# Setup of weight-derived constants moved from ahead of a branch into its arms

## The chip, the cores and the metric

The kernel runs on one core of one Trainium2 chip. The metric is the device time in microseconds of one execution. Three runs of the kernel before took 4162.62, 4162.65 and 4139.63 us (median 4162.62). The execution that the profile shows took 4152.3 us, and its span, from the first to the last instruction, is 4150.5 us. A core has five engines that are meant here by PE (TensorE, with PEld for its weight loads), DVE (VectorE), ACT (ScalarE), POOL (GpSimd) and SP (SyncE, which issues DMAs). ACT issues DMAs too, on a queue of its own.

## The reference

The input x is 32 sequences of 256 tokens with 256 features. The output is x + FFN(Cond(x, cond)).

Cond is a state-space block:

```python
xr, gate = split(x @ W_in.T)                 # 512 channels each
xc = silu(causal_conv4(xr + cond) + b_conv)
xn = layernorm(xc) * ln_g + ln_b
Bm, Cm, dt = split(xn @ W_xproj.T, 3)        # 16 states each
dt = tanh(dt @ W_dt.T + b_dt) * 0.01
Ad = 1 - dt * tanh(A_log)
Bd = Bm * min(norm(xn), 1)
h[t] = clip(h[t-1] * Ad[t] + Bd[t] * xn[t], -10, 10)
y[t] = Cm[t] . h[t] + D * xn[t]
out = (y * silu(gate)) @ W_out.T
```

FFN has two layers. Each is a local attention (8 heads of 64, a token shift, normalised and rotated q and k, window 128) and a gated feed-forward block with a layer norm, each with a residual.

## The kernel before, in words

The 32 sequences go in four groups of 8. For each group the state-space block is a scan over 256 steps in 8 chunks of 32. One step is one DVE instruction (`h`, line 576) on 128 rows (16 states by 8 sequences) and 512 channels. Its input `xrep` is a row of normalised x, spread over the 128 rows either by a DMA out of a DRAM scratch `xnd` (lines 465 and 550) or, in group 0 alone, by a small matmul (`bx`, line 558), and scaled on ACT by `beta` (line 569). After the scan of a group come two layers of attention and feed-forward. The scan of group g + 1 runs beside the layers of group g (`side_by_side`). Only group 0 has its scan to itself, at the start, and only the last group has its layers to itself, at the end.

The scan's work is written into an agenda: `at(s, what, ...)` puts a piece at step s, and the pieces are traced in the order of the steps, those of one step in the order in which they were added. Pieces of chunk c have steps around 32c, those that prepare it negative offsets. For chunk 0 the order is: load of x (`load_x`, step −43), input projection (`project`, −40 to −34, PE `ps_in`, line 333), convolution (`conv_in`, `conv_taps`, `conv_out`, −38 to −29; POOL does the first tap `acc`, line 369, DVE the others), the projections of the raw convolution output on the states (`raw_sums`, −26, PE `ps_raw` from `wx_sb`), the norm (`norm_turn` to `norm_out`, −24 to −12; statistics on DVE, the power of −0.5 on POOL at line 444, `xn` on ACT, gain and bias on POOL at lines 460 and 461, then the write to `xnd` and the square on ACT), `figures` and `figures_in` (−9 and −7, these read `wsum` and `wbias`), `decays` (−5, reads `a_sb`), then the steps from 0 on. `skip` multiplies with `dskip_sb` (line 618), `project_y` uses `w_out_sb`, and the gate's pieces use the second half of the input projection.

The written order is not the issue order. A planner orders each engine's instructions from dependencies, from the priority that the written order gives, and from its own estimate of when operands are there; an instruction that needs nothing can be issued well ahead of its place. `tc.keep_in_program_order` ties an instruction behind the one written before it on its engine in the same block. Buffers come from pools; tiles with one tag share that tag's buffers. `ap_` has the tags `rot` (4 buffers) and `swp` (3 buffers) of 128x512. In the scan of group 0 `rot` holds the tiles `xq`; both tags serve attention later. `ps_w` has 8 banks of PSUM.

Two versions of the program exist in one kernel, behind a test at run time. `bounded` is 1 when the scales of q and k are small enough to do without the maximum in the softmax; every engine reads it and takes one arm of `tc.If`. Nothing in an arm is issued ahead of that. Ahead of the test lies the setup. It loads the weights and constants, mostly on ACT's queue (`loaded`, lines 110 to 120), and computes from them:

- masks, selectors and identity matrices, from nothing (POOL and DVE);
- `a_sb` = −0.01 tanh(A_log) (lines 168 and 169), `w_out_sb` halved (line 172), `head_rows` (line 197);
- rotation tables `rc_sb` and `rs_sb` times the scales (lines 219 to 233, DVE, line 229);
- `bounded` (lines 235 to 244, DVE);
- `wx_sb`, which is W_xproj with W_dt folded into its last third and the norm's gain folded in: four times a transpose (line 258), a copy, a product with W_dt (line 262) and a copy (lines 256 to 265);
- `wsum` and `wbias`, the sums that let the norm be applied after the projection: six times a copy that repeats 16 columns 8 times (`wide`, 128x512, DVE, line 269), four matmuls with 2 columns (`tw`, line 272, two records each in the profile) and a copy (lines 267 to 280).

Of the kernel before, what the change touches and what calls it, by code (L numbers as in the profile page):

```python
# [10 lines left out]
FP = mybir.dt.float32  # L11
BF = mybir.dt.bfloat16
I32 = mybir.dt.int32
AF = mybir.ActivationFunctionType
ALU = mybir.AluOpType
AX = mybir.AxisListType
PSUM = bass.MemoryType.PSUM
DRAM = bass.MemoryType.DRAM

P = 128  # L20
S = 256
DM = 256
KM = DM // P
DI = 512
NC_ = DI // P
NS = 16
GB = 8
# [9 lines left out]
HEADS = 8  # L37
DH = 64
W = 128
NW = S // W  # L40
HID = 682
MCH = [(o, min(P, HID - o)) for o in range(0, HID, P)]
MREM = MCH[-1][1]
# [6 lines left out]
SCALES2 = 25.0  # L50


def bc(ap, axis, n):

    ap = ap.unsqueeze(axis)
    shape = list(ap.shape)
    shape[axis] = n
    return ap.broadcast_to(shape)
# [15 lines left out]
def kernel(  # L74
# [29 lines left out]
    nc = tc.nc  # L104
    B = xT.shape[2]
    L = wqkv.shape[1]
    NG = B // GB

    const = ctx.enter_context(tc.tile_pool(name="const", bufs=1))
    def loaded(src, shape, name, q=None):  # L110
        t = const.tile(shape, FP, tag=name, name=name)
        (q or nc.scalar).dma_start(out=t, in_=src)
        return t

    def per_state(src, name):
# [3 lines left out]
        nc.scalar.dma_start(out=t, in_=src)  # L119
        return t  # L120

    w_in_sb = loaded(w_inT, [P, KM, 2 * DI], "w_in_sb", nc.sync)
    cond_sb = loaded(condT, [P, NC_, B], "cond_sb")
    wc_sb = loaded(w_conv, [P, NC_, TAPS], "wc_sb")
    bconv_sb = loaded(b_conv, [P, NC_], "bconv_sb")
    lng_sb = loaded(s_ln_g.partition_broadcast(P), [P, DI], "lng_sb")
    lnb_sb = loaded(s_ln_b.partition_broadcast(P), [P, DI], "lnb_sb")
    dskip_sb = loaded(d_skip.partition_broadcast(P), [P, DI], "dskip_sb")
    w_out_sb = loaded(w_outT, [P, NC_, DM], "w_out_sb")
    flg_sb = loaded(f_ln_g, [P, L, KM], "flg_sb")  # L130
    flb_sb = loaded(f_ln_b, [P, L, KM], "flb_sb")
    b1_sb = loaded(b1, [P, L, 2, len(MCH)], "b1_sb")
    b2_sb = loaded(b2, [P, L, KM], "b2_sb")
    bdt_sb = per_state(b_dt, "bdt_sb")
    a_sb = per_state(a_log, "a_sb")

    ident = const.tile([P, P], FP, tag="ident", name="ident")
# [17 lines left out]
    for j in range(NJ):  # L155
# [9 lines left out]
    nc.gpsimd.memset(half, 0.5)  # L165


    nc.scalar.activation(a_sb, a_sb, AF.Tanh)
    nc.vector.tensor_scalar(a_sb, a_sb, -1.0, 0.01, ALU.mult, ALU.mult)


    nc.vector.tensor_scalar(w_out_sb, w_out_sb, 0.5, None, ALU.mult)

    mask_t = const.tile([P, 2 * W], BF, tag="mask_t", name="mask_t")
    ident_b = const.tile([P, P], BF, tag="ident_b", name="ident_b")
# [3 lines left out]
        out=mask_t[:, 0:W], in_=mask_t[:, 0:W], compare_op=ALU.is_ge, fill=MASKED_LOW,  # L181
# [3 lines left out]
        out=mask_t[:, W : 2 * W], in_=mask_t[:, W : 2 * W], compare_op=ALU.is_ge,  # L185
# [6 lines left out]
    head_rows = const.tile([P, HEADS, DH], FP, tag="head_rows", name="head_rows")  # L192
    for r in range(2):
        nc.gpsimd.memset(head_cols[:, r, r * 16 : (r + 1) * 16], 1.0)
    for h in range(HEADS):
        row = 32 * (h // 2) + 16 * (h % 2)
        nc.vector.tensor_copy(
            head_rows[:, h, :], ident[:, row : row + 1].broadcast_to([P, DH])
        )

    b1g_sb = const.tile([P, L], FP, tag="b1g_sb", name="b1g_sb")
    nc.scalar.dma_start(
        out=b1g_sb[DH : DH + MREM], in_=b1[0:MREM, :, 1, len(MCH) - 1]
    )

    bounded = const.tile([1, 1], I32, tag="bounded", name="bounded")

    rc_sb = const.tile([P, L, NW, 2, DH], FP, tag="rc_sb", name="rc_sb")
    rs_sb = const.tile([P, L, NW, 2, DH], FP, tag="rs_sb", name="rs_sb")


    wx_sb = const.tile([P, NC_, 4 * NS], FP, tag="wx_sb", name="wx_sb")

    wsum = const.tile([P, 3], FP, tag="wsum", name="wsum")
    wbias = const.tile([P, 3], FP, tag="wbias", name="wbias")
    with tc.tile_pool(name="setup", bufs=2) as setup, tc.tile_pool(
        name="setup_ps", bufs=2, space=PSUM
    ) as sps:

        for src, pos, dst in ((qk_scale, rot_c, rc_sb), (qk_scale_sw, rot_s, rs_sb)):  # L220
            tab = setup.tile([P, NW, 2, DH], FP, tag="tab", name="tab")
            nc.scalar.dma_start(out=tab, in_=pos)
            for l in range(L):
                sc = setup.tile([P, 2 * DH], FP, tag="qk_sc", name="qk_sc")
                nc.scalar.dma_start(
                    out=sc, in_=src[l].rearrange("a d -> (a d)").partition_broadcast(P)
                )
                for w in range(NW):
                    nc.vector.tensor_mul(
                        dst[:, l, w].rearrange("p a d -> p (a d)"),  # L230
                        tab[:, w].rearrange("p a d -> p (a d)"),
                        sc,
                    )

        sq = setup.tile([1, L, 2, DH], FP, tag="sq", name="sq")
        nc.scalar.dma_start(out=sq, in_=qk_scale.unsqueeze(0))
        nc.vector.tensor_mul(sq, sq, sq)
        big = setup.tile([1, L, 2], FP, tag="big", name="big")
        nc.vector.tensor_reduce(big, sq, AX.X, ALU.max)
        nc.vector.tensor_mul(big[:, :, 0], big[:, :, 0], big[:, :, 1])  # L240
        nc.vector.tensor_scalar(big[:, :, 1], big[:, :, 0], SCALES2, None, ALU.is_le)
        allb = setup.tile([1, 1], FP, tag="allb", name="allb")
        nc.vector.tensor_reduce(allb, big[:, :, 1], AX.X, ALU.min)
        nc.vector.tensor_copy(bounded, allb)

        wx0 = setup.tile([P, NC_, 3 * NS], FP, tag="wx0", name="wx0")
        nc.scalar.dma_start(out=wx0, in_=w_xT)
        wdt_sb = setup.tile([NS, NS], FP, tag="wdt", name="wdt_sb")
        nc.scalar.dma_start(out=wdt_sb, in_=w_dtT)
        gcol = setup.tile([P, NC_], FP, tag="gcol", name="gcol")  # L250
        nc.scalar.dma_start(out=gcol, in_=s_ln_g.rearrange("(c p) -> p c", p=P))

        cols = setup.tile([P, NC_, 2], FP, tag="cols", name="cols")
        nc.gpsimd.memset(cols[:, :, 0:1], 1.0)
        nc.scalar.dma_start(out=cols[:, :, 1], in_=s_ln_b.rearrange("(c p) -> p c", p=P))
        for c in range(NC_):
            td = sps.tile([P, P], FP, tag="td", name="td")
            nc.tensor.transpose(td[0:NS, :], wx0[:, c, 2 * NS : 3 * NS], ident)
            wdT = setup.tile([NS, P], FP, tag="wdT", name="wdT")
            nc.vector.tensor_copy(wdT, td[0:NS, :])  # L260
            td2 = sps.tile([P, P], FP, tag="td", name="td2")
            nc.tensor.matmul(td2[:, 0:NS], wdT, wdt_sb, start=True, stop=True)
            nc.vector.tensor_copy(wx0[:, c, 2 * NS : 3 * NS], td2[:, 0:NS])
        nc.gpsimd.memset(wx_sb, 0.0)
        nc.vector.tensor_mul(wx_sb[:, :, 0 : 3 * NS], wx0, bc(gcol, 2, 3 * NS))
        for i in range(3):
            for src, k, dst in ((wx_sb, 0, wsum), (wx0, 1, wbias)):
                wide = setup.tile([P, NC_, NS, GB], FP, tag="wide", name="wide")
                nc.vector.tensor_copy(wide, bc(src[:, :, i * NS : (i + 1) * NS], 3, GB))
                tw = sps.tile([P, 2], FP, tag="tw", name="tw")  # L270
                for c in range(NC_):
                    nc.tensor.matmul(
                        tw,
                        wide[:, c].rearrange("p n b -> p (n b)"),
                        cols[:, c, :],
                        start=(c == 0),
                        stop=(c == NC_ - 1),
                    )
                nc.vector.tensor_copy(dst[:, i : i + 1], tw[:, k : k + 1])
        nc.vector.tensor_add(wbias[:, 2:3], wbias[:, 2:3], bdt_sb)  # L280

# [1 line left out]
    for i in range(2):  # L285
        t = const.tile([P, NI * (P + GB)], FP, tag=f"ly{i}", name=f"ly{i}")
# [3 lines left out]
    def program(ctx, exact):  # L290
# [7 lines left out]
        ap_ = ctx.enter_context(tc.tile_pool(name="at", bufs=2, reuse_waits="tile"))  # L298
        aw = ctx.enter_context(tc.tile_pool(name="aw", bufs=3, reuse_waits="tile"))
        ps_w = ctx.enter_context(tc.tile_pool(name="psw", bufs=8, space=PSUM, reuse_waits="tile"))  # L300

        def bank(pool, tag, name):
            return pool.tile([P, DI], FP, tag=tag, name=name)

        def reorder(out, ps):

# [5 lines left out]
        def group_scan(g, ys):  # L312
# [13 lines left out]
            def at(s, what, *args):  # L326
                agenda.setdefault(s, []).append(partial(what, *args))
# [376 lines left out]
            at(-1, start)  # L704
            if alone:
                at(-30, spread_weights)
            for c in range(NCH):
                for t in range(CH):
                    at(c * CH + t, step, c, t)
# [136 lines left out]
        if exact:  # L846
# [4 lines left out]
                out=mask[:, 0:W], in_=mask[:, 0:W], compare_op=ALU.is_ge, fill=MASKED,  # L851
# [449 lines left out]
        for _ in group_scan(0, ys):  # L1301
            pass
# [5 lines left out]
        for g in range(NG):  # L1308
# [12 lines left out]
            at = state_at[0]  # L1321
# [119 lines left out]
```

## Time and profile before

| | |
|---|---|
| median of 3 runs | 4162.62 us (4139.63 to 4162.65) |
| profiled execution | 4152.3 us |
| its span | 4150.5 us, 51929 instructions |
| mean granted TensorE clock | 0.959 |
| PE / DVE / ACT / POOL busy | 91% / 63% / 44% / 41% |
| `bounded` written, arm's first instruction (SP) | 22.3 us, 22.9 us |
| first `ps_in` on PE | 37.3 us |
| first and last scan step of group 0 begin | 69.6 us, 464.1 us |

Busy shares are means over the whole span. In the scan of group 0 alone, POOL is busy for about 19 of 47 us per chunk and DVE for about 40. Every row of a timeline gives the start, the duration, the engine, the line, the operation with its result and its operands, the shapes, the number of instructions merged into the row, and in brackets the idle time of the engine before it and what ended it. A name with a q after the engine (ACTq, SPq) is the engine's sequencer, which issues DMAs. Windows give busy times of each engine in a stretch, then the granted clock, the share of the DMA engines and GB/s.

### The profile page before, as it was taken

The numbers are of one execution on the slowest core, as the hardware profiler recorded it, in microseconds if no ns is written. First come the engines' busy times: TensorE is split into PE (matmuls) and PEld (weight loads), VectorE is DVE, ScalarE is ACT, GpSimd is POOL, SyncE is SP. The second block draws the span as 40 slices with busy tenths as digits, with TensorE's granted clock in tenths as the row PEclk, the third lists the DMA queues.
The fourth block names the chain that finished last, engine by engine and source line by source line (L and its number), as shares of the span: only waits on it lengthen the run. The fifth ranks groups of instructions, "written<-read, shape, count | busy, mean of one in ns | idle before, by whom it ended". The sixth has DMA issues, their size and how long they took to land. (4 is left out here: it accounts for less than half of the span.)

```text
span 4150.5 us, 51929 instructions
## 1 busy us (share of the span) xinstructions
PE 3797.3 (91%) x18236; PEld 2008.9 (48%) x18236; DVE 2627.6 (63%) x4986; ACT 1810.9 (44%) x3345; POOL 1699.9 (41%) x1749
## 2 busy tenths in 40 slices
PE   5898898899989999899898999889998899999999
PEld 3333355544555455444455445554455545654653
DVE  5888567777766456767767636777776744434433
ACT  2655344545445334444544424454544533323331
POOL 3333265325543166423654136532554316513531
PEclk8988899999999999999999999999999999999999
DMA  4444312444335312444433421244433421000000
GB/s 118 123 113 113 80 44 72 128 120 119 92 84 146 81 44 76 114 111 120 106 88 113 124 65 44 75 127 119 119 90 91 139 77 37 8 14 22 1 11 32
DMA packets 257346, 353.10 MB, mean 85 GB/s; under 512 B 160867, under 2 KB 170420, under 8 KB 254900
## 3 DMA queue, kind: packets, MB, share of 16 engines
q1 hardware_dynamic: 172624, 337.67, 29.8%
q10 hardware_dynamic: 84452, 12.01, 1.9%
q8 instruction: 147, 2.41, 0.3%
q14 instruction: 123, 1.01, 0.1%
HBM read 314.49 MB, written 33.55 MB: 84 GB/s over the span
## 5 line engine op out<-in xcount | busy, mean ns | idle before, releaser
L576 DVE CUSTOM_DVE_ANT_0 h<-h,xrep,lim 128x512 f32<-128x512 f32 x1024 | 894.7, 874 | 82.5 <-PE y L588 23.3
L569 ACT ACTIVATE xrep<-xrep,beta 128x512 f32<-128x512 f32 x896 | 609.4, 716 | 771.2 <-DMA xrep<-xnd 702.6
L786 PE MATMUL ps_qkv<-wqkv_sb,res 128*128 128x512 f32 x1536 | 750.2, 628 | 32.5 <-ACT oT L1036 8.2
L810 POOL TENSOR_TENSOR rot<-rot,swp 128x512 f32<-128x512 f32 x256 | 327.4, 1279 | 655.1 <-DVE swp L807 597.8
L786 PEld LDWEIGHTS ps_qkv<-wqkv_sb,res 128*128 128x128 f32 x1536 | 290.5, 199 | 386.9 <-issue 304.9
L818 POOL TENSOR_TENSOR rn<-ss,neg_half 128x8 f32<-128x8 f32 x256 | 436.7, 1706 | 23.3 <-DVE ss L816 11.7
L802 DVE TENSOR_TENSOR rot<-ps_qkv,rc_sb 128x512 f32<-128x512 f32 x256 | 175.7, 686 | 393.3 <-ACT sq L799 392.9
L1145 PE MATMUL po_f<-ag,w_sb 128*128 128x512 f32 (+1 forms) x768 | 358.9, 618 | 21.6 <-DVE ag L1126 21.5
L588 PE MATMUL y<-h,ly 128*32 128x512 f32 x2048 | 362.0, 631 | 14.3 <-DVE h L576 13.1
L1116 PE MATMUL pa<-hT,w_sb 128*128 128x512 f32 (+1 forms) x896 | 364.0, 597 | 0.0
L1126 DVE SCALAR_TENSOR_TENSOR ag<-pa,b_sb,gl 128x512 f32<-128x512 f32 x192 | 143.5, 748 | 320.3 <-PE pa L1116 147.5
L1116 PE MATMUL pg<-hT,w_sb 128*128 128x512 f32 x640 | 309.8, 607 | 0.3 <-ACT gl L1124 0.3
L333 PE MATMUL ps_in<-xg,w_in_sb 128*128 128x256 f32 x1024 | 291.1, 414 | 12.8 <-issue 4.5
L819 POOL TENSOR_TENSOR rot<-rot,rn 128x512 f32<-128x512 f32 x256 | 280.1, 1094 | 19.0
L380 DVE SCALAR_TENSOR_TENSOR acc<-xr,wc_sb,acc 128x256 f32<-128x256 f32 x384 | 199.4, 523 | 111.1 <-POOL acc L369 108.5
L1079 POOL TENSOR_TENSOR rstd<-ve,neg_half 128x1 f32<-128x1 f32 x128 | 77.9, 609 | 467.3 <-DVE ve L1077 461.6
L333 PEld LDWEIGHTS ps_in<-xg,w_in_sb 128*128 128x128 f32 x1024 | 191.0, 201 | 156.0 <-issue 71.9
L1000 ACT ACTIVATE pT<-sc 128x512 f32<-128x512 f32 x384 | 206.1, 592 | 127.4 <-PE sc L991 114.0
L836 PE MATMUL ps_wo<-oT,wo_sb 128*128 128x256 f32 x1024 | 237.3, 385 | 0.0
L1145 PEld LDWEIGHTS po_f<-ag,w_sb 128*128 128x128 f32 (+1 forms) x768 | 135.4, 191 | 203.1 <-issue 133.5
L799 ACT ACTIVATE sq<-ps_qkv 128x512 f32<-128x512 f32 x256 | 148.1, 592 | 187.0 <-PE ps_qkv L786 141.5
L991 PE MATMUL sc<-qT,kT 64*128 64x128 f32 (+1 forms) x2048 | 227.1, 352 | 1.9 <-ACT kT L830 1.8
(152 smaller groups left out, 5615.2 us busy)
## 6 DMA issues: line engine op xcount, KB each, us to landing
xrep<-xnd SPq DMA_DIRECT2D x448, 512.0 KB
xnd<-xn SPq DMA_DIRECT2D x64, 256.0 KB
wqkv_sb<-in_wqkv_dram SPq DMA_DIRECT2D x8, 1536.0 KB
xd<-xnd SPq DMA_DIRECT2D x192, 64.0 KB
w_sb<-in_w_dram SPq DMA_DIRECT2D x8, 1364.0 KB
xg<-in_xT_dram SPq DMA_DIRECT2D x64, 128.0 KB
ys<-yo ACTq DMA_DIRECT2D x64, 128.0 KB
res<-ys SPq DMA_DIRECT2D x32, 256.0 KB
```

Of the source, the lines that this page charges most:

```text
L333: nc.tensor.matmul(ps, w_in_sb[:, k, ch * P : (ch + 1) * P], ck[c]["xg"][:, k], start=(k == 0), stop=(k == KM - 1),)
L569: nc.scalar.activation(bx, ck[c].pop(("bx", t), bx), AF.Copy, scale=ck[c]["beta"][:, t : t + 1])
L576: nc.vector._custom_dve(TENSOR_ADD_SAT, out=h_new, in0=state["h"], in1=bx, s0=ck[c]["lim"][:, 0, t : t + 1], s1=ck[c]["lim"][:, 1, t : t + 1],
L588: nc.tensor.matmul(ck[c]["y", hb][32 * q : 32 * q + 32, :], ly[hb % 2][:, 32 * t : 32 * t + 32], ck[c].pop(("h", hb * TB + t)), start=(i = ...
L786: nc.tensor.matmul(ps, res[b // 2][:, k, b % 2, t0 : t0 + W], wqkv_sb[:, k, a * DI : (a + 1) * DI], start=(k == 0), stop=(k == KM - 1),)
L810: nc.gpsimd.tensor_add(rot, rot, swp)
L818: nc.gpsimd.tensor_tensor(rn, ss, neg_half, ALU.pow)
L819: nc.gpsimd.tensor_mul(rot, rot, bc(rn, 2, DH))
L836: nc.tensor.matmul(po[:, d], wo_sb[:, c, d * P : (d + 1) * P], oT[:, c, :], start=(c == 0), stop=(c == NC_ - 1),)
L991: nc.tensor.matmul(banks[r][:, i, :], kT[rows, i0 + i, kw * W : (kw + 1) * W], qT[rows, i0 + i, kw * W :], start=False, stop=(i == n - 1),)
L1116: nc.tensor.matmul(ps[0:n, :], self.w1[:, k, half_ * HID + o : half_ * HID + o + n], self.h[j][:, k].rearrange("p b t -> p (b t)"), start= ...
L1145: nc.tensor.matmul(self.po[d], self.w2[r0 : r0 + n, m, d * P : (d + 1) * P], self.ag[m][r0 : r0 + n, :], start=(m == 0), stop=(m == len(MC ...
```

## The change

The test moves forward: the load of the scales and the chain that computes `bounded` come first, ahead of all other loads, with the load on SP's queue. Seven loads (`dskip_sb`, `w_out_sb`, the norms' and the feed-forward's constants) and all that the setup computes from weights, except `bounded`, move into the arms as pieces of the agenda of group 0. They get work tiles of `rot` and `swp` in place of the setup's own pool and PSUM banks of `ps_w`, whose pool of the setup goes.

| step | piece | engine |
|---|---|---|
| −43 | `load_w`: four loads, two fills | ACT queue, POOL |
| −34, −32 | `fold_1`, `fold_2`: the four transposes into one bank and one copy, four products and one copy, then `wx_sb` | PE, DVE |
| −28 to −18 | `widen_w`, six, 128x512 | POOL, in written order (before: DVE) |
| −27 to −17 | `sum_w`, six, four matmuls each, into one bank | PE |
| −19 | `decay_rate` | ACT, DVE |
| −16 | `load_later`: the seven loads | ACT queue |
| −14 | `sums_w`: two copies and an addition | DVE |
| 14 | `halve`, 128x1024 | POOL, in written order (before: DVE) |
| 30 | `load_tables`: six loads | ACT queue |
| 50 to 68 | `tables`, four, 128x256 each | POOL, in written order (before: eight on DVE) |
| 100 to 114 | `head_table`, eight, 128x64 | POOL, in written order (before: DVE) |

The removed parts of the setup are those that the list of the previous section names; the core of what is added:

```diff
+    bounded = const.tile([1, 1], I32, tag="bounded", name="bounded")
+    with tc.tile_pool(name="setup", bufs=1) as setup:
+        sq = setup.tile([1, L, 2, DH], FP, tag="sq", name="sq")
+        nc.sync.dma_start(out=sq, in_=qk_scale.unsqueeze(0))
...
+        nc.vector.tensor_copy(bounded, allb)
+
     w_in_sb = loaded(w_inT, [P, KM, 2 * DI], "w_in_sb", nc.sync)
...
-    dskip_sb = loaded(d_skip.partition_broadcast(P), [P, DI], "dskip_sb")
-    w_out_sb = loaded(w_outT, [P, NC_, DM], "w_out_sb")
-    flg_sb = loaded(f_ln_g, [P, L, KM], "flg_sb")
-    flb_sb = loaded(f_ln_b, [P, L, KM], "flb_sb")
-    b1_sb = loaded(b1, [P, L, 2, len(MCH)], "b1_sb")
-    b2_sb = loaded(b2, [P, L, KM], "b2_sb")
...
+        def constants(at):
+            tmp = {}
+            def work(tag, name, bufs):
+                return ap_.tile([P, HEADS, DH], FP, tag=tag, name=name, bufs=bufs).rearrange(
+                    "p h d -> p (h d)"
+                )
+            def load_w():
+                w = work("rot", "wx", 4)
...
+                nc.scalar.dma_start(out=tmp["wx"], in_=w_xT)
+                nc.scalar.dma_start(out=tmp["dt"], in_=w_dtT)
+                nc.scalar.dma_start(out=tmp["g"], in_=s_ln_g.rearrange("(c p) -> p c", p=P))
+                nc.scalar.dma_start(
+                    out=tmp["cols"][:, :, 1], in_=s_ln_b.rearrange("(c p) -> p c", p=P)
+                )
+                nc.gpsimd.memset(tmp["cols"][:, :, 0], 1.0)
+                nc.gpsimd.memset(wx_sb, 0.0)
+            def fold_1():
+                td = bank(ps_w, "w", "td")
+                for c in range(NC_):
+                    nc.tensor.transpose(
+                        td[0:NS, c * P : (c + 1) * P], tmp["wx"][:, c, 2 * NS :], ident
+                    )
+                wdT = work("swp", "wdT", 3)
+                nc.vector.tensor_copy(wdT[0:NS], td[0:NS])
...
+            def widen_w(i, k):
+                t = ap_.tile([P, NC_, NS, GB], FP, tag="swp", name="wide", bufs=3)
+                src = (wx_sb, tmp["wx"])[k]
+                tc.keep_in_program_order(
+                    nc.gpsimd.tensor_copy(t, bc(src[:, :, i * NS : (i + 1) * NS], 3, GB))
+                )
+                tmp["wide"] = t
...
+            def halve():
+                tc.keep_in_program_order(
+                    nc.gpsimd.tensor_scalar_mul(w_out_sb, w_out_sb, 0.5)
+                )
+            def load_tables():
+                tab, sc = work("swp", "tab", 3), work("swp", "qk_sc", 3)
...
+            def tables(i, l):
+                dst = (rc_sb, rs_sb)[i][:, l].rearrange("p w a d -> p w (a d)")
+                tc.keep_in_program_order(
+                    nc.gpsimd.tensor_mul(dst, tmp["tab"][:, i], bc(tmp["sc"][:, i, l], 1, NW))
+                )
...
+            at(-43, load_w)
+            at(-34, fold_1)
+            at(-32, fold_2)
+            for n in range(6):
+                at(-28 + 2 * n, widen_w, n // 2, n % 2)
+                at(-27 + 2 * n, sum_w, n // 2, n % 2)
+            at(-14, sums_w)
+            at(-19, decay_rate)
+            at(-16, load_later)
+            at(14, halve)
+            at(30, load_tables)
+            for n in range(2 * L):
+                at(50 + 6 * n, tables, n // L, n % L)
+            for h in range(HEADS):
+                at(100 + 2 * h, head_table, h)
...
             if alone:
                 at(-30, spread_weights)
+                constants(at)
```

## The prediction

> **What bounds the kernel now.** First the page, for the whole span:
>
> ```profile
> span 4150.5 us, 51929 instructions
> ...
> PE 3797.3 (91%) x18236; PEld 2008.9 (48%) x18236; DVE 2627.6 (63%) x4986; ACT 1810.9 (44%) x3345; POOL 1699.9 (41%) x1749
> ```
>
> TensorE is busy for 91% of the span, so work taken from VectorE or GpSimd in the middle of the program is worth nothing there. But the change rewrites the first microseconds, so the view that decides is the timeline from 0 to 130 us (start, duration, engine, line, operation):
>
> ```profile
> 17.14 0.32 ACTq L236 DMA_DIRECT2D sq<-in_qk_scale_dram  x1
> ...
> 20.11 0.41 DVE L237 TENSOR_TENSOR sq<-sq 1x256 f32<-1x256 f32 x1
> ...
> 22.13 0.13 DVE L244 CAST bounded<-allb 1x1 int32<-1x1 f32 x1
> ...
> 22.93 2.61 SPq L346 DMA_DIRECT2D xg<-in_xT_dram  x4
> ...
> 25.59 0.95 SPq L1195 DMA_DIRECT2D wqkv_sb<-in_wqkv_dram  x1
> ...
> 27.09 10.37 PE L272 MATMUL tw<-cols,wide 128*128 128x2 f32 x48 [1.23 <-issue]
> ...
> 37.32 6.03 PE L333 MATMUL ps_in<-xg,w_in_sb 128*128 128x256 f32 x16
> ...
> 45.85 1.33 POOL L369 TENSOR_SCALAR acc<-xr,wc_sb,bconv_sb 128x256 f32<-128x256 f32 x2
> ...
> 49.02 0.60 POOL L362 COPY xr<-carry 128x24 f32<-128x24 f32 x2 [1.84 <-DVE acc L380]
> ...
> 53.09 1.08 POOL L444 TENSOR_TENSOR stat<-ve,neg_half 128x1 f32<-128x1 f32 x2 [3.47 <-DVE ve L443]
> ```
>
> Two gates stand in a row. The arms open when `bounded` is written (22.26); its input was asked for only at 17.14, behind some twenty other loads on ACT's queue, and the arm's first instruction follows at 22.93. Then the first projection `ps_in` waits again, not for data: TensorE has 48 `tw` matmuls of the setup ahead of it. The DMA view of 24 to 26 us shows that its input was there by then, since the 2048 short packets of the first chunk's two `xg` loads are all in this stretch (counts are packets, MB, share):
>
> ```profile
> q1 hardware_dynamic: 2051, 0.26, 82.4%
> ```
>
> So `ps_in` could have begun near 26 and began at 37.3. From there to the first scan step is a chain of latencies (convolution, transpose, statistics, affine, write and re-read of `xnd`), as VectorE's timeline from 60 us and the busy times by window show (PE, PEld, DVE, ACT, POOL, clock, DMA share, GB/s):
>
> ```profile
> 69.62 0.81 DVE L576 CUSTOM_DVE_ANT_0 h<-h,xrep,lim 128x512 f32<-128x512 f32 x1
> ```
>
> ```profile
> 50.00:60.00 10.00, 1.62 (x8) 0.83 (x8) 2.27 (x9) 2.55 (x6) 6.08 (x6) 0.78 0.11 32
> 60.00:70.00 10.00, 7.95 (x28) 5.58 (x30) 5.91 (x21) 2.71 (x6) 4.43 (x11) 0.70 0.51 144
> ```
>
> TensorE is idle for 8.4 of the 10 us after 50: whatever shortens the way to 69.62 shortens the program.
>
> **The change, step by step**, against the profiled execution (4152.3 us, 1.8 around its span).
>
> 1. *The gate.* The load of `sq` takes the first place on SP, where `w_in` is issued now (0.74 us). Issue to use of `sq` was 20.11 − 17.14 = 3.0 us, an upper bound, VectorE having been busy until 20.1. That gives 3.7. The chain to `bounded` took 2.15 with other work between (1.4 by its rows alone), the arm 0.67 more: the arm opens near 6.2 to 6.6. The other engines are there: GpSimd's fills end at 3.9, less the two that move; ACT keeps 7 of its loads, whose issues end near 4.6 (the pause of 2.15 us that I see came behind the eighth); VectorE's remaining sums and copies, 1.9 us, fit while `sq` travels. Gain 22.9 − 6.4 = **16.5 us**.
> 2. *TensorE's queue.* `ps_in` waits for `xg`, 3.1 us after the arm's start by the row above. At 6.4 the last of `w_in`, `lng` and `lnb` and the moved `wx`, `g`, `cols` travel too, so I add 0.5: `ps_in` at 10.0, not 37.3. Steps 1 and 2 are **−27.3** in all. The bounds are −28.5 (nothing collides) and −22 (the fold's transposes are put ahead of `ps_in` and wait for `wx` among the weights' 4.2 MB).
> 3. *The fold on TensorE and VectorE.* 8 records of transposes (0.38) and 8 of products (0.38) cost at most 6 us if each stands alone, but now go in two batches with one round trip each, inside the lead-in, where TensorE is idle after `ps_in`. VectorE adds 0.28–0.45 + 0.2 + 0.36, about 1 us, between convolution taps that are the path. The 48 `tw` records (0.216 us apart) lie in TensorE's idle time; if they had no cover they would cost 10.4. Cost **+1**, ends 0 and +4.
> 4. *Six widening copies on GpSimd.* No row shows a GpSimd copy of 128x512. Below stands the fill of 128x544 (0.55), above the two-input 128x512 of L460 (1.26). Twice the one-input 128x256 of L369 (0.64) is 1.27; I take 1.1, nearest to the one-input row. They total 6.6, ends 3.3 and 7.6. By the order that the pins write, four stand behind the last `acc` and ahead of the first power, where GpSimd is idle from 47.2 to 53.1 but for 0.6: covered. The other two stand between the first power and the second half's affine, where GpSimd works back to back from 54.8 to 60: 2.2, less 0.6 of idle. Cost **+1.6**, ends 0 and +7.6 (no cover).
> 5. *ACT's loads.* The seven deferred loads took about 5 us to issue (0.45, 0.45, 0.34, 1.35, 0.93 for two, 1.43). They depend on nothing, and row L1195 shows that such loads go out as soon as the arm opens, whatever their place in the program. ACT idles until its first `th`, some 7 us behind `ps_in`; the four `wx` loads and these fill 6.7 of its 10. Cost **+0.5**, ends 0 and +5 (issued between `xn` and its square, on the path).
> 6. *In the scan that runs alone.* Halving 128x1024 (some 2.2 by the rows of 4), four 128x256 products (0.65) and eight head copies (0.2 each by L362) are 6.4 us on GpSimd, which is busy 19 of 47 us per chunk there and mostly waits for VectorE. Six table loads take ACT 2.5 us. Cost **+1**, ends 0 and +7. VectorE loses 3.7 us of setup rows that were ahead of both gates and are already counted.
>
> Sum: −27.3 + 1 + 1.6 + 0.5 + 1 = **−23 us**, ends −28.5 and about −10. From the profiled execution that is 4129; from the median of the runs (4162.62) 4140, from their lowest (4139.63) 4117. I say **4133**, between the first two.
>
> [...] The six copies: DVE does one in 0.42 us by its row L269, GpSimd's one-input row is 0.64 for half the size. [...] The clock: the 16 `ps_in` behind `tw` average 558 ns where the run's shortest is 379, so they were already slow. [...]
>
> **Rivals.**
>
> *The constants become the chain* (0.15). `wide`, `wdT` and the tables share the three `swp` buffers. If the tables' loads, which need nothing, take two of them at the arm's start and keep them, the copies run singly: 6 × (1.1 + 1.73 of `tw` + 0.3) = 19 us from the last `acc`, 10 behind `ps_in`, to 29, while `figures_in` needs the sums at 26 (63.5 − 37.3). With ACT's issues on the path too that is some 8 to 10 us lost: −13, 4139 by the profiled execution. For it: loads do float (L1195). Against: TensorE is free meanwhile.
>
> *The arms don't open early* (0.05): an engine reaches the branch late, as ACT did with its queue full, or one of its loads is held. At 12 us instead of 6.4, the gain is 17: 4135.
>
> *More than 1% faster* (0.13). The direct gain ends at 28.5 us, 0.7%. It needs runs like the lowest before: 4139.6 − 23 = 4117, or a start-up that is warm as well (from 80 to 90 us the clock is 0.68 and TensorE full: 3 us).
>
> *Slower* (0.06). One mechanism: no pin holds TensorE, ACT or VectorE, and the order of the later instructions is planned from the new start; if that order feeds the scan later, each step pays. The page has 82.5 us of idle time before the 1024 `h` steps, 0.08 us each. At 0.022 us more for each the 23 us are gone, at 0.063 the program is 1% slower: 4152 − 23 + 64 = 4193. For it: `h` waits 9.0 us for ACT's `xrep` in the first 600 us already. Against: the moved work is done before step 116 of the first 256, and the other three groups have the same instructions as before.
>
> The forecast itself has the rest, 0.61. The range reaches from the lowest base with most of the gain (4139.6 − 28.5 = 4111, and a little for the faster case) to the median with nothing gained: **4105 to 4163**. 1% of 4162.62 is 41.6 us, about what a measurement of this kernel can tell from no change; by the cases: faster 0.13, within 1% 0.81, slower 0.06.
>
> **What the profile afterwards would show.** Right: `bounded` near 6 us, the first `ps_in` near 10 with no `tw` ahead of it, the first `h` step near 45.4 (69.6 − 27.3 + 3.1, step 6 coming later), and the same distance from there to the end. Step 4 is right if GpSimd's copies are about 1.1 us and the first power follows the last `acc` by some 6 us. Step 5 is wrong if ACT's queue shows loads between `xn` and `sq_x`; the first rival is right if each `wide` waits for the `tw` before it. The slower case would show as more idle time before L576. I am wrong in sign if the distance from the first `h` step to the end grows by more than 23 us.

## The result, and the profile after

| | before | after |
|---|---|---|
| median of 12 runs each | 4159.07 us (4139.63 to 4167.02) | 4142.44 us (4132.39 to 4154.91) |
| ratio | | 0.9971, 95% interval 0.9953 to 0.9989 |
| profiled execution, its span | 4152.3 us, 4150.5 us | 4133.24 us, 4131.4 us |
| first `ps_in` | 37.32 us | 10.43 us |
| last `xc` ends | 50.25 us | 26.23 us |
| last `tp_x` ends | 51.62 us | 35.80 us |
| first scan step | 69.62 us | 54.51 us |

The change makes the kernel faster by 0.29%, some 12 us by the ratio and 16.6 by the medians. In a later comparison on one chip, with five runs of it, the ratio was 0.9965 (0.9952 to 0.9979), 15.6 us by the medians. The forecast was 23 us, a ratio of 0.9945: the direction held, and the size is beyond the interval. That the time itself, 4133, met the profiled execution (4133.24) is luck: this was the second fastest of the 12.

The page of the changed kernel, its first line and the busy times of the whole span, says nothing of this:

```profile
span 4131.4 us, 51897 instructions
...
PE 3798.7 (92%) x18236; PEld 2010.1 (49%) x18236; DVE 2621.9 (63%) x4953; ACT 1812.4 (44%) x3345; POOL 1716.0 (42%) x1768
```

TensorE is as busy as before (3797.3 us there); the 19 us are idle time that is gone. The timeline of the changed kernel from 3 to 56 us shows where it went and where some came back (start, duration, engine, line, operation; in brackets the idle time before it and what ended it):

```profile
3.83 0.14 DVE L134 CAST bounded<-allb 1x1 int32<-1x1 f32 x1
...
6.31 1.01 SPq L419 DMA_DIRECT2D xg<-in_xT_dram  x2
...
10.43 5.80 PE L406 MATMUL ps_in<-xg,w_in_sb 128*128 128x256 f32 x12 [10.43 <-DMA xg<-in_xT_dram]
...
20.37 0.35 DVE L283 TENSOR_TENSOR wx_sb<-wx 128x192 f32<-128x192 f32 x1
...
23.03 1.86 PE L300 MATMUL tw<-wx,wide 128*128 128x2 f32 x8 [3.42 <-POOL wide L289]
24.83 2.82 PE L472 MATMUL ps_raw<-xc,wx_sb 128*64 128x256 f32 x6
...
25.81 0.42 DVE L463 SCALAR_TENSOR_TENSOR xc<-th,acc 128x256 f32<-128x256 f32 x1 [0.55 <-ACT th L458]
...
27.57 1.87 PE L300 MATMUL tw<-wx,wide 128*128 128x2 f32 x8
29.30 0.88 PE L502 MATMUL tp_x<-ident,xc 128*128 128x128 f32 x3
29.98 3.41 PE L300 MATMUL tw<-wx,wide 128*128 128x2 f32 x16
33.25 0.88 PE L502 MATMUL tp_x<-ident,xc 128*128 128x128 f32 x3
34.06 1.12 PE L472 MATMUL ps_raw<-xc,wx_sb 128*64 128x256 f32 x2
35.11 0.69 PE L502 MATMUL tp_x<-ident,xc 128*128 128x128 f32 x2
...
35.62 1.30 DVE L512 BATCH_NORM_STATS2 st<-tp_x 128x6 f32<-128x512 f32 x2 [9.39 <-PE tp_x L502]
...
54.51 0.89 DVE L649 CUSTOM_DVE_ANT_0 h<-h,xrep,lim 128x512 f32<-128x512 f32 x1
```

Both gates are open: `bounded` is written at 3.97, the load of x leaves at 6.31, and `ps_in` begins at 10.43 with no `tw` ahead of it. But 32 of the 48 `tw` records now stand between the projection and the last transpose `tp_x`, and the first of them keeps TensorE waiting for a copy on GpSimd. TensorE kept to that order: `ps_raw`, which stands next, had its first `xc` at 18.83 and its `wx_sb` at 20.72 and begins at 24.83, behind the first eight, though TensorE idled for 3.42 us ahead of these. VectorE's statistics, which are the path, wait 9.39 us for the transposes. In the timeline of the kernel before, the same wait was 1.19:

```profile
49.43 0.82 DVE L390 SCALAR_TENSOR_TENSOR xc<-th,acc 128x256 f32<-128x256 f32 x2
...
50.96 0.66 PE L429 MATMUL tp_x<-ident,xc 128*128 128x128 f32 x4
...
51.44 1.29 DVE L439 BATCH_NORM_STATS2 st<-tp_x 128x6 f32<-128x512 f32 x2 [1.19 <-PE tp_x L429]
```

In numbers, from the first `ps_in` to the first scan step: 32.3 us before, 44.1 after. Of the 11.8 more, 2.9 lie ahead of the last `xc` (15.8 against 12.9), 8.2 between it and the last `tp_x` (9.6 against 1.4), and 0.7 behind that (18.7 against 18.0). So of the 26.9 us that the gates give, 15.1 are left at the first scan step.

### The profile page after: what moved, and what is told of

Read it like the earlier page. It is cut to its first block, busy times and chain, and to the rows that moved or that the text cites. A ratio compares the mean times of both kernels' runs of the same rounds, so it can differ in the third digit from the quotient of the medians.

```text
span 4131.4 us, 51897 instructions
## 1 busy us (share of the span) xinstructions
PE 3798.7 (92%) x18236; PEld 2010.1 (49%) x18236; DVE 2621.9 (63%) x4953; ACT 1812.4 (44%) x3345; POOL 1716.0 (42%) x1768
## 5 line engine op out<-in xcount | busy, mean ns | idle before, releaser
L892 POOL TENSOR_TENSOR rn<-ss,neg_half 128x8 f32<-128x8 f32 x256 | 437.2, 1708 | 23.2 <-DVE ss L890 11.8
L406 PE MATMUL ps_in<-xg,w_in_sb 128*128 128x256 f32 x1024 | 289.2, 411 | 21.6 <-DMA xg<-in_xT_dram 10.4
```

Of the source, the lines that this page charges most:

```text
L406: nc.tensor.matmul(ps, w_in_sb[:, k, ch * P : (ch + 1) * P], ck[c]["xg"][:, k], start=(k == 0), stop=(k == KM - 1),)
L892: nc.gpsimd.tensor_tensor(rn, ss, neg_half, ALU.pow)
```

## The experiments

The theory after the result, called O in what follows, was the order: the planner put the sums' matmuls ahead of the transposes in TensorE's queue, and the transposes wait behind them as `ps_raw` does (ready at 20.72, begun at 24.83). Its rival C was the clock: in the window from 20 to 40 us of the changed kernel the granted clock is 0.50, so that TensorE might have been late whatever the order.

**The gate alone.** The chain of `bounded` moves to the front of the kernel before; all else stays.

```diff
+    bounded = const.tile([1, 1], I32, tag="bounded", name="bounded")
+    with tc.tile_pool(name="gate", bufs=1) as setup:
+        sq = setup.tile([1, L, 2, DH], FP, tag="sq", name="sq")
+        nc.sync.dma_start(out=sq, in_=qk_scale.unsqueeze(0))
...
-        sq = setup.tile([1, L, 2, DH], FP, tag="sq", name="sq")
-        nc.scalar.dma_start(out=sq, in_=qk_scale.unsqueeze(0))
```

> The kernel before with one edit: the load and the chain of `bounded` stand first; all other setup stays ahead of the arms, on the engines where it was. My account (two gates in a row, steps 1 and 2 of the prediction): the arm's first instruction on SP comes near 6 us instead of 22.9, but TensorE still has the fold and the 48 `tw` records ahead of `ps_in`, so `ps_in` begins between 33 and 38 us and the first `h` step between 65 and 70; the time does not change by more than the runs scatter. Rival (the branch alone was the gate): `ps_in` begins near 21 us and the first `h` near 54, as in the changed kernel.

Measured: 4158.38 us in one run, beside 4155.85 of the kernel before. Its timeline:

```profile
3.47 0.14 DVE L133 CAST bounded<-allb 1x1 int32<-1x1 f32 x1
...
15.89 5.10 SPq L347 DMA_DIRECT2D xg<-in_xT_dram  x4
...
28.05 10.37 PE L273 MATMUL tw<-cols,wide 128*128 128x2 f32 x48 [1.23 <-issue]
38.29 5.22 PE L334 MATMUL ps_in<-xg,w_in_sb 128*128 128x256 f32 x16
...
70.61 0.81 DVE L577 CUSTOM_DVE_ANT_0 h<-h,xrep,lim 128x512 f32<-128x512 f32 x1
```

`bounded` is there at 3.6. SP asks for x only at 15.89, not near 6 as expected; why stays open. It makes no difference, since `ps_in` waits for the setup's matmuls as before. It begins at 38.29 and the first scan step at 70.61, both just above the ranges expected. The prediction's two gates stand in a row, and the first is worth nothing by itself. (The second alone was not run.)

**The sums behind the transposes.** On the changed kernel, the six `sum_w` are tied behind what is written before them on TensorE, none earlier than step −19, the second half of the norm. For that, three of the `wide` tiles go to the tag `rot`.

```diff
-                    nc.tensor.matmul(
+                    tc.keep_in_program_order(nc.tensor.matmul(
...
-                at(-27 + 2 * n, sum_w, n // 2, n % 2)
+                at(max(-19, -27 + 2 * n), sum_w, n // 2, n % 2)
```

> The changed kernel with the `sum_w` matmuls written at steps -19 and -17, behind the second `norm_turn`, and tied there in written order; three of the six `wide` tiles take `rot` buffers so that no copy waits for a sum. Theory O (order): the `tw` records stand ahead of the transposes `tp_x` in TensorE's queue and hold the norm back; here the last transpose ends 1 to 3 us behind the last `xc` instead of 9.6, and the first `h` step comes at 46 to 48 us instead of 54.5; the time falls by 7 to 8 us against the changed kernel, ratio to the kernel before near 0.995. Theory C (clock): the stage is long because TensorE runs at half clock from 20 to 50 us; then the transposes stay slow and the first `h` stays within 2.5 us of 54.5.

Measured: 4134.37 us, ratio 0.9943 (0.9929 to 0.9956). By the ratio that is 24 us below the kernel before, by the medians 21.5; the forecast had 23. Its timeline:

```profile
22.44 1.12 PE L508 MATMUL tp_x<-ident,xc 128*128 128x128 f32 x4
...
27.00 0.44 PE L508 MATMUL tp_x<-ident,xc 128*128 128x128 f32 x2
27.27 9.73 PE L305 MATMUL tw<-wx,wide 128*128 128x2 f32 x48
...
47.67 0.89 DVE L655 CUSTOM_DVE_ANT_0 h<-h,xrep,lim 128x512 f32<-128x512 f32 x1
```

All 48 records follow the last transpose, which ends at 27.4, 1.1 us behind the last `xc`. The first scan step is at 47.67, 6.8 us earlier than with the change as it is. The matmuls themselves are the same and take about as long (9.73 us for the 48, and 10.87 in the five rows of the changed kernel); only their place differs. The clock does not stay the same in this profile, though: the records give full clock from 24.4 to 27.8, where the last transposes run, and half clock over the same stretch in the changed kernel. The second profile of this kernel, further below, settles it. There the clock is at half from 21.7 to 45.6, and still the last transpose ends 1.8 us behind the last `xc` (9.6 in the changed kernel), and the first scan step is at 48.93. C is refuted as the main cause.

From the last transpose to the first scan step this kernel takes 20.2 us, though, against 18.7 in the changed kernel. Much of that is ACT's queue:

```profile
28.55 0.34 ACTq L345 DMA_DIRECT2D tab<-in_rot_c_dram  x1
28.99 2.02 ACTq L493 DMA_DIRECT2D rw<-raw  x3
31.06 0.78 ACT L532 ACTIVATE xn<-tp_x,stat 128x512 f32<-128x512 f32 x1 [3.58 <-DMA tab<-in_rot_c_dram]
```

The first table load, written for step 30, now stands ahead of the write of `raw` and of `xn`, which begins 0.9 us after its statistics are there (30.15); 1.4 us in the second profile. In the changed kernel that load is issued behind `xn`.

**A quarter of each sum.** One of the four matmuls of each sum is left, so three quarters of what `wsum` and `wbias` add up are left out.

```diff
-                for c in range(NC_):
+                for c in range(1):
```

> The changed kernel with one of the four matmuls of each `sum_w` kept (three quarters of the sums are left out of the computation). Theory O: 18 of the 24 `tw` records that stand ahead of the last transpose go, 0.216 us each, so the first `h` comes 4 to 6 us earlier, near 49 to 50. Theory C: within 2.5 us of 54.5.

Measured: 4130.26 us in one run, first scan step at 47.88, last `tp_x` at 29.1 instead of 35.8. With 12 records in place of 48 in the same places the lag behind the last `xc` falls to 2.5 us, and the first step comes 6.6 us earlier, a little more than the 4 to 6 expected; the clock, at full from 26.9 to 33.7 here, may have a part in that. The first `tw` still waits 3.41 us for GpSimd's copy, so this wait by itself is not what holds the last transpose back. It says the same by another way: what delays the path is TensorE time in front of the transposes.

**Small sums.** The sums are taken on the 16 columns themselves (48x2 and so on), and three matmuls with a repeating identity spread the result over 128 rows. The six copies on GpSimd go.

```diff
-            for n in range(6):
-                at(-28 + 2 * n, widen_w, n // 2, n % 2)
-                at(-27 + 2 * n, sum_w, n // 2, n % 2)
+            at(-43, repeater)
+            at(-27, sum_w)
+            at(-19, repeat_w)
```

> The changed kernel with the sums made another way: eight matmuls give the sums of the 48 columns as they are (48 rows by 2), one VectorE copy, then three matmuls with a constant repeating matrix spread them to 128 rows, tied behind the transposes. No `wide` copies on GpSimd, 22 records in place of 48. Theory O: the first `h` comes at 45 to 47 us, and the time 8 to 10 us under the changed kernel, ratio to the kernel before near 0.994. Theory C: the first `h` stays near 53, since GpSimd's copies cost about 1 us of the path.

Measured: 4137.57 us, ratio 0.9954 (0.994 to 0.9967), first scan step at 47.73, just behind the 45 to 47 expected. From the last `tp_x` to that step it takes 18.2 us, against 18.7 in the changed kernel and 18.0 in the kernel before, so the copies cost some 0.5 there. But the last transpose ends at 29.53, 2.1 us later than with the sums late, and again a table load in ACT's queue has a part in it:

```profile
20.99 0.34 ACTq L352 DMA_DIRECT2D tab<-in_rot_c_dram  x1
21.37 0.42 ACT L471 ACTIVATE th<-acc 128x256 f32<-128x256 f32 x1 [3.50 <-DMA w_out_sb<-in_w_outT_dram]
...
21.82 0.43 DVE L476 SCALAR_TENSOR_TENSOR xc<-th,acc 128x256 f32<-128x256 f32 x1 [2.75 <-ACT th L471]
```

ACT's second `th`, at 17.86 with the sums late, begins at 21.37 behind that load, VectorE waits 2.75 for it, and the last `xc` ends 1.0 us later. The rest lies between the last `xc` and the last transpose, presumably by the 16 `ts` records ahead of `ps_raw`. As a remedy this version is no better than the order alone.

**The same kernels again.** The changed kernel and the kernel before were profiled a second time.

> The changed kernel once more, for a second profile. The order of TensorE's queue is fixed, so the first scan step should again be near 54.5 us (within 1.5), 9 to 10 us behind its place without the sums in front. The half clock of the last chunk (27 us long in the first profile, steps 224 to 240 in some 28 us) either recurs, then it belongs to the kernel, or is 3.4 us (20.4 us for those steps), then it is scatter between executions.

> The kernel before once more, for a second profile. First scan step near 69.6 us (within 1.5). The half clock of the last chunk of the lone scan was 3.4 us in its first profile: if it is 27 to 37 us here, the 8 to 13 us that the changed kernel lost there between the profiles were scatter; if it is 3.4 us again, they may belong to the change.

Measured: 4136.46 us after, 4171.31 before, one run each. The first scan steps are at 54.66 and 69.65, within 0.2 us of the first profiles: the start repeats. What follows does not. Windows of the kernel before, first and second profile, over the end of group 0's scan (busy us of PE, PEld, DVE, ACT, POOL, then the granted clock, DMA share, GB/s):

```profile
410.00:430.00 20.00, 15.99 (x61) 4.05 (x60) 18.03 (x34) 12.38 (x24) 6.10 (x8) 0.91 0.59 158
430.00:450.00 20.00, 20.00 (x77) 7.94 (x76) 15.11 (x20) 12.64 (x23) 1.29 (x1) 1.00 0.51 119
```

```profile
410.00:430.00 20.00, 16.01 (x43) 4.14 (x44) 15.20 (x30) 10.28 (x19) 3.88 (x6) 0.57 0.55 141
430.00:450.00 20.00, 20.00 (x36) 4.93 (x34) 8.95 (x11) 4.31 (x7) 1.68 (x2) 0.58 0.20 54
```

TensorE is busy for the same time and does 79 matmuls in place of 138, at a clock of 0.57 to 0.58 in place of 0.91 to 1.00. From the first to the last step of group 0's scan the two executions of one kernel take 394.5 and 405.2 us. The changed kernel took 397.3 and 400.8. Steps 224 to 240 hold the difference before, with 20.4 and 31.9 us; after they took 27.8 both times. So the long half clock recurs in the changed kernel, but the kernel before can have it too, and worse. It doesn't belong to the change, though two profiles of each don't tell how often each has it. Over this stretch a comparison of two single profiles is worth nothing below some 10 us.

**Warmth at the start.** On the kernel with the sums late, 24 matmuls of the identity with itself stand ahead of `ps_in`, to see whether its records are slow because TensorE idled before them.

```diff
+            def warm():
+                b = bank(ps_w, "w", "warm")
+                for _ in range(24):
+                    tc.keep_in_program_order(
+                        nc.tensor.matmul(b[:, 0:P], ident, ident, start=True, stop=True)
+                    )
...
+                at(-43, warm)
```

> Built on e2_sums_late. 24 matmuls of 128x128 on the identity, results never read, stand ahead of the first input projection, in TensorE's idle time from 5 to 10 us. [...] If the filler is too long, the projection starts later than 10.4.

Measured: 4126.90 us in one run. The extra matmuls end at 12.6, so `ps_in` begins 2.3 us late, but its first 12 records take 2.76 us instead of 4.97, and it ends at 16.68 against 16.60. Behind 48 records in a row the projection is not slow; behind an idle TensorE it was. (With the sums late alone the trace has no clock record before 14.2 us, so the records' own times tell it: seven of the 12 take 634 ns or more and the last three 379, and here all take 379 to 382.) The first scan step is at 49.75. The low time of this run comes from group 0's scan, which took 388.9 us, and is one run.

**A filler in the scan.** On the kernel with the sums late, three matmuls of 128x512 stand at the end of each chunk of group 0's scan, ahead of the first transpose of the output, where TensorE idled some 2.6 us.

```diff
+            def fill():
+                b = bank(ps_w, "w", "fill")
+                for _ in range(3):
+                    tc.keep_in_program_order(
+                        nc.tensor.matmul(b, ident, w_in_sb[:, 0, 0:DI], start=True, stop=True)
+                    )
...
+                    if alone and hb == 0:
+                        at(s + 22, fill)
```

> Built on e2_sums_late. In the scan that group 0 has to itself, TensorE idles some 2.6 us at the end of each chunk (its first transpose of the output waits for VectorE), and the records show stretches of half clock, each a multiple of 3.41 us, that recur every 51.2 us. Here three matmuls of 128x512 (six records, some 2.6 us, their results never read) stand ahead of that transpose in each of the 8 chunks. Theory G (the idle gap is what drops the clock, and the half clock slows the scan): the stretches vanish or shorten, mean clock up from 0.955 by some 0.005 to 0.01, and the way from the first to the last scan step of group 0 shrinks from some 402 us by 10 to 25; total 4110 to 4125 by a base of 4135. Rival F (the clock does not follow this gap): the stretches stay, the filler adds 0 to 2 us per chunk; total 4135 to 4150.

Measured: 4127.41 us, ratio 0.992 (0.9908 to 0.9932), a little above the total that G named; group 0's scan took 384.6 us, 17.9 less than in the first profile of the kernel with the sums late, which G expected.

**Four on one chip.** The changed kernel, the sums late, the filler, and the filler with 13 of the warming matmuls, five runs each (four of the last), against the same runs of the kernel before (4157.15 us).

> The changed kernel beside the three that follow, so that all four stand against the same runs of the kernel before. Theory O (the order of TensorE's queue at the start is what is missing from the forecast): ratio 0.996 to 0.998, 10 to 15 us above the kernel with the sums behind the transposes.

> The kernel of e2_sums_late once more, on the same chip as the changed kernel. Theory O: ratio 0.993 to 0.995, median 8 to 13 us below the changed kernel. If the first interval was luck, the two medians lie within 4 us.

> The kernel of e5_fill once more. Theory G (TensorE's idle gap at the end of a chunk drops the clock of the scan that runs alone): 6 to 12 us below the kernel with the sums late, ratio 0.991 to 0.993. Rival (it was scatter of the clock between executions): within 4 us of it.

> The filler in the scan and, at the start, 13 of the matmuls of e8_warm (26 records) in place of 24, so that they end at about 10 us, before the input is there. If warmth at the start is worth something by itself, the projection's first 12 records take some 2.8 us in place of 5, the first scan step comes 1.5 to 2.2 us earlier than 47.7, and the time is 1 to 3 us below the kernel with the filler alone; if not, both are equal.

| kernel | median us | ratio (95%) | first scan step | group 0's scan |
|---|---|---|---|---|
| changed | 4141.56 | 0.9965 (0.9952 to 0.9979) | 51.66 | 401.1 |
| sums late | 4132.20 | 0.9939 (0.9925 to 0.9952) | 48.93 | 398.0 |
| sums late, filler | 4121.64 | 0.9908 (0.9893 to 0.9923) | 49.09 | 388.2 |
| sums late, filler, warm | 4120.04 | 0.9908 (0.9893 to 0.9923) | 47.95 | 388.7 |

The order of the sums is worth 9.4 us by the medians, within the 8 to 13 that O said of one kernel and just below the 10 to 15 that it said of the other; by the two intervals that has some 8 us of uncertainty either way. The first scan step, which is where the order acts, has 2.7 us of it in this pair of profiles, and 6.8 in the pair before. The changed kernel's first step is 3 us earlier here than in its other two profiles with the same order of instructions: the clock rose for part of the queue (eight `tw` took 1.16 us at 27.4, not 1.87), and the statistics waited 6.4 us for the transposes, not 9.4. So the loss by the order was itself scaled by the clock.

The filler is worth 10.6 us more, at the upper end of what G said. Windows of the kernel with the sums late and of the one with the filler, over the scan of group 0, columns as above:

```profile
50.00:440.00 390.00, 351.87 (x1280) 132.15 (x1276) 330.53 (x589) 222.89 (x411) 147.50 (x181) 0.89 0.45 114
```

```profile
50.00:440.00 390.00, 352.01 (x1348) 137.32 (x1344) 340.63 (x599) 225.80 (x415) 147.49 (x182) 0.92 0.45 116
```

TensorE is busy equally long in both, with the filler's 48 records inside. The granted clock is 0.92 instead of 0.89, which over 390 us is 11.7 us of full clock. But the stretches of half clock do not vanish; together they are shorter, 61 us instead of 85 in this window. And the first profile of the kernel before has 0.92 in its scan without a filler, so the clock of a single execution proves nothing; the rounds carry this verdict.

Nor does the filler take TensorE's idle time away. TensorE's rows at the end of a chunk, without the filler and with it:

```profile
388.45 1.09 PE L722 MATMUL tz<-ident,xd 128*128 128x128 f32 x4 [2.60 <-DVE xd L716]
...
392.82 1.14 PE L564 MATMUL ps_st<-rhs,sel 128*128 128x96 f32 x4 [1.44 <-DVE rhs L563]
```

```profile
381.12 2.84 PE L786 MATMUL fill<-w_in_sb,ident 128*128 128x512 f32 x6
383.80 0.62 PE L722 MATMUL tz<-ident,xd 128*128 128x128 f32 x4
388.17 1.14 PE L564 MATMUL ps_st<-rhs,sel 128*128 128x96 f32 x4 [3.74 <-DVE rhs L563]
```

The idle time moves from `tz` to `ps_st`, and the half clock moves with it: here it begins 1.5 us ahead of `tz` without the filler and 3.8 behind it with the filler. In these two profiles the 9.8 us that the scan gains lie in its first 32 steps (4.6) and its last 32 (5.3); the six chunks between them take 299.3 us in both. So the gain in time is measured, but that the filler brings it by closing the gap is not shown, and how it shortens the stretches was not settled.

The warming matmuls do what they should. PE rows of the kernel with filler and warmth:

```profile
4.84 4.50 PE L786 MATMUL warm<-ident 128*128 128x128 f32 x26 [4.84 <-POOL wx L259]
10.47 0.70 PE L412 MATMUL ps_in<-xg,w_in_sb 128*128 128x256 f32 x2 [1.13 <-DMA xg<-in_xT_dram]
11.67 2.43 PE L412 MATMUL ps_in<-xg,w_in_sb 128*128 128x256 f32 x10 [0.49 <-DMA xg<-in_xT_dram]
```

The first 12 records take 3.6 us from the first to the last, 0.49 of it a wait for the second part of x, where the filler alone has 5.41. The last `xc` ends at 25.22, against 26.37 to 26.70 in the four profiles with the sums late and no warming. The first scan step, at 47.95, is 1.1 us earlier than with the filler alone, but those four profiles have 47.67 to 49.09; it was expected 1.5 to 2.2 us ahead of 47.7. The total is 1.6 us lower by the medians, which is inside the intervals. This version, at 4120 us some 0.9% below the kernel before, is the fastest of the study; it is not distinguished from the filler alone.

## Why the prediction was right and where it was not

*The two gates* (steps 1 and 2) were right in their sum: the arm's first instruction on SP at 6.3 (forecast 6.2 to 6.6), `ps_in` at 10.43 (forecast 10.0), −26.9 us (forecast −27.3). Two misses cancel in it, which is luck: `bounded` was there at 4.0, not near 6, and SP followed 2.3 us later, not 0.67 (GpSimd at 4.7). The pause in ACT's loads that the working names stood behind the seventh load, not the eighth; the seven loads kept were issued by 4.4. The gate alone showed that the first is worth nothing without the second.

*Step 3 failed*, in its sentence "The 48 `tw` records (0.216 us apart) lie in TensorE's idle time; if they had no cover they would cost 10.4. Cost +1, ends 0 and +4." The mechanism of the prediction stands, and this term of its sum was mis-sized. TensorE has idle time in that stretch, but the records were not put into it. They are in the queue ahead of `ps_raw` and `tp_x`, which are the path. Measured: 8.2 us in the profile between the last `xc` and the last `tp_x` (about 5 in the profile whose clock was higher: 32.55 − 26.01 = 6.5 against 1.4), and 9.4 us, less surely, by the medians on one chip. With them moved, the change brings about what the sum had, by the medians 25.0 us on that chip and 21.5 on another (25 and 24 by the ratios), and the first scan step is at 47.7 to 48.9 where 45.4 was forecast. The bound of 10.4 "without cover" was in the working and was not taken into the ends. The fold, the rest of step 3 (with the later half of x), cost up to 2.9 ahead of the last `xc`, inside its ends, where +1 was taken.

*The total.* The worst ends of the steps add up to +1.6 us, not to the "about −10" of the sum. And 4133 is 29.6 us below the median that it stood against, 6.6 more than the sum: it came from a base between the profiled execution and the median, for which no step gives a reason.

*Step 4* was right in sign and somewhat high. Timeline of the changed kernel, GpSimd:

```profile
22.92 0.80 POOL L289 COPY wide<-wx 128x512 f32<-128x512 f32 x1
...
37.27 0.56 POOL L517 TENSOR_TENSOR stat<-ve,neg_half 128x1 f32<-128x1 f32 x1 [10.97 <-DVE ve L516]
37.78 0.61 POOL L289 COPY wide<-wx_sb 128x512 f32<-128x512 f32 x1
38.35 0.56 POOL L517 TENSOR_TENSOR stat<-ve,neg_half 128x1 f32<-128x1 f32 x1
```

A copy took 0.61 to 0.80 us, not the estimated 1.1. Four are covered on GpSimd, and two stand where they were forecast, one of them between the powers: +0.7 from the last `tp_x` to the scan here, against +1.6. The sign that was to show it, a first power some 6 us behind the last `acc`, came only with the sums late (6.8 us); here it is 15.0, since the power waits for the transposes. The cover was argued on GpSimd alone, though. TensorE, which waits for these copies, had none.

*The clock at the start.* The prediction took the 16 records of `ps_in` for slow already, 558 ns in the mean where the shortest is 379. That holds as far as it goes: with the change they take 588 ns in the first profile, hardly more. But the runs with warming matmuls show that they need not be slow: 12 records in 3.6 instead of 5.41 us. In the first profile of the changed kernel the records of `ps_in` take 634 ns or more up to 15.6 and 379 to 382 from 16.65 on; the clock is at full from 16.40, 6.0 us behind the first matmul (10.43). There was warmth to be won, 1.2 to 1.5 us at the last `xc`; at the first scan step it is not told from the scatter of single profiles.

*Step 5* was right for the seven loads. The last of them is issued by 16.3, and ACT's first `th` at 17.55 waits for VectorE. What the prediction took for the sign of an error, loads between `xn` and `sq_x`, is there all the same: the table loads of step 6 come as early as 39.22, but `sq_x` waits for GpSimd then. Where the order of the sums was changed, one of them did hold ACT back, as shown above. ACT's timeline in the changed kernel:

```profile
14.89 1.42 ACTq L324 DMA_DIRECT2D b1g_sb<-in_b_dram  x1
17.55 0.81 ACT L458 ACTIVATE th<-acc 128x256 f32<-128x256 f32 x2 [6.92 <-DVE acc L453]
```

*Step 6* can't be told from nothing: from step 32 to step 224, which hold the tables and the head copies, the scan took 298.9 us after and 300.1 before. The halving, 3.21 us for 128x1024 at 75.35, is longer than the 2.2 that was taken, and a chunk is 49.3 us in the mean before, not 47.

*The rivals.* The arms do open early. The constants don't become a chain through the `swp` buffers: one `wide` waits 0.56 us for a `tw` before it. Yet the time is near that rival's (−13), by another mechanism. Slower by a worse-fed scan did not come: from the first to the last of the 1024 steps the changed kernel took 3289.7, 3295.1 and 3299.2 us in its three profiles, the kernel before 3294.4 and 3312.4.

## What to carry to other kernels

Work that is moved out of a setup into the path has to be placed on every engine that it uses. Here GpSimd's part was held in order and TensorE's was left to a planner, which put the moved matmuls ahead of the path in TensorE's queue (`ps_raw`, ready at 20.72, begins at 24.83) and gave back a third of 25 us, more or less. When a forecast covers moved work with "the engine is idle there", ask what stands behind it in that engine's queue and whether it can be held; where it can't, the uncovered price belongs into the range.

## What was not expected of the hardware

The granted clock of TensorE falls to half in the middle of group 0's scan, where TensorE is busy for 90% of the time (350.75 of the 390 us from 70 on in the kernel before). In the records of that scan such stretches last a multiple of 3.41 us: 3.41, 10.24 and 13.65 in the kernel before, 3.41 to 27.31 in the changed kernel. From 205.88 on they begin 51.2, 54.6, 51.2 and 51.2 us after the one before in the kernel before, and from 146.10 on 44.4 to 58.0 in the changed kernel, which is about the length of a chunk (49.3). They go with TensorE's idle time: in the first profiles of these two kernels, from 100 to 430 us, each begins between 1.8 us before and 0.8 us after the end of an idle gap of 2.6 to 3.0 us, except one of 3.41 us that follows a gap by 6.5. Over all 14 profiles it is up to 1.7 us after, gaps of up to 3.7 us, and a few such exceptions. That is a coincidence in time; what sets their length is open. The one in the last chunk was 3.4 us long in three profiles (before, the quarter sums, the warmed start), and 20 to 38 us in the eleven others. Without a filler the long ones cost steps 224 to 240 between 7 and 13 us (27.8 in the changed kernel, 33.5 with the sums late in their first profile, 20.4 in the kernel before). This is one source of the scatter between executions of one kernel: of the 18.9 us between the two profiled executions of the kernel before, group 0's scan holds 10.7.
